# Layer 1, block 0: the causal mask added on TensorE, and one maximum for two heads

## The chip, the cores and the metric

The kernel runs on one core of one Trainium2 chip. Its time is the device time in microseconds (us) of one execution; the profile is of one execution more, whose own time is given beside its span, the time from its first to its last instruction. The engines are TensorE (PE for products, PEld for the loads of their stationary side), VectorE (DVE), ScalarE (ACT), GpSimd (POOL) and SyncE (SP), which issues most DMAs.

## What is computed

Two transformer layers over 2048 tokens of 128 channels. Layer 0 has attention of 16 heads without a mask and a mixture of 16 experts beside a shared one; layer 1 has causal attention of 8 heads with one set of keys and values for all, and a feed-forward part. The change is in layer 1's attention:

```python
k = x @ Wk
v = x @ Wv
q = jnp.einsum('btc,qcd->bqtd', x, Wq)
wei = jnp.einsum('bqtd,bsd->bqts', q, k) * scale
causal = jnp.tril(jnp.ones((t, t), dtype=bool))
wei = jnp.where(causal, wei, -jnp.inf)
wei = jax.nn.softmax(wei, axis=-1)
out = jnp.einsum('bqts,bsd->btqd', wei, v)
```

## The kernel before

Both attentions are made by one function, `attention` (from L319), which works in 4 blocks of 512 queries and, in each, in groups of 4 heads. A block and a group are a unit: layer 1 has 8 units, two to a block. Every unit goes through the keys twice.

The first pass finds the largest score of each query (`first_pass`, L396). One step (`step`, L402) takes a tile of 128 queries, a block of up to 512 keys and a pair of heads. Two products at L411 write the pair's scores into the two halves of a PSUM tile, one in the array's upper 64 rows and the other in its lower 64; the operands are in the reduced 32-bit format, with a high and a low part stacked along the rows. VectorE then takes the maxima. Where the keys lie wholly ahead of the queries, one plain reduction (L415) does both heads. Where the keys are of the queries' own block (`own`), the scores of later keys must not count. Then only the first n keys are multiplied, n being 128, 256, 384 or 512 for the four query tiles of a block, and each head gets an operation of its own at L420: it adds a strip of the constant `later` (L130 to L133), which is zero up to the diagonal and -2^100 after it, and takes the maximum. Its result comes through an accumulator, so that each L420 is followed by a short read of that accumulator. In block 0 every step is of this second kind, 8 steps to a unit.

The unit's maxima are then combined and negated (L426), split into a high and a low part (L436, L437), transposed on TensorE (L444) and copied by ScalarE (L445). The second pass (`second_pass`, L455) makes the scores again with keys as rows (L476), subtracts the maximum with one more product (L482), takes the exponential on ScalarE (L486), zeroes what lies after the diagonal on GpSimd (L489) and weighs the values on TensorE (L502).

PSUM tiles for scores come from one pool of three (`ps_s`), used by both passes in turn, so TensorE can be at most three pairs ahead of VectorE and ScalarE. The first pass of the next unit is woven into the second pass of the present one (`look_ahead`). In block 0 of layer 1 the first unit has nothing before it to be woven into: its 8 steps run with only the preparation of block 1 among them. This preparation is the keys (L295, finished by L296 and L297), the queries (L382, split at L272 and L273, and stacked by DMAs on SP's queue at L290) and the values (L1127, L1128).

Some stages carry an order written out by hand, but that ends with `ordered.close()` just ahead of layer 1's attention. From there on the build's scheduler decides how each engine's instructions stand. Constants are made at the start: `ident`, `later`, zeros and counters by GpSimd.

Of the kernel before, what the change touches and what calls it, by code (L numbers as in the profile page):

```python
# [11 lines left out]
F32R = mybir.dt.float32r  # L12
# [7 lines left out]
P = 128  # L20
T = 2048
NT = T // P
QB = 512
# [20 lines left out]
def two_layers(ctx: ExitStack, tc: tile.TileContext, a: dict, out: bass.AP):  # L44
    nc = tc.nc
    const = ctx.enter_context(tc.tile_pool(name="const", bufs=1))


    ident = const.tile([P, P], F32, name="ident")
# [67 lines left out]
    def gates(layer):  # L117
        for j in (2, 5):
# [11 lines left out]
    later = const.tile([P, QB], F32, name="later")  # L130
    nc.gpsimd.memset(later, 0.0)
    nc.gpsimd.affine_select(out=later, in_=later, compare_op=ALU.is_ge, fill=MASKED,
                            base=QB - P, pattern=[[-1, QB]], channel_multiplier=1)  # L133

    low = const.tile([P, 2, 2], F32, name="low")
    for i, at in enumerate((ident.rearrange("p (r c) -> p r c", c=4)[:, :, 2:4],
# [180 lines left out]
    def attention(layer, hT, ngrp, dk, scale, causal, kvp, begin, prepare, wq, bq, folded, ended,  # L317
# [23 lines left out]
        with ExitStack() as s:  # L341
# [10 lines left out]
            def other_bank():  # L352
                nonlocal others
                others += 1
                return banks[(weighing + 1 if fused or weighing >= 0 else others) % 2]
# [42 lines left out]
            def first_pass(u):  # L398

                b, grp = units[u]  # L400
                pm = qp.tile([P, TB, HG, NB], F32, name=f"{L}mx{u}", tag="mx")
                nkb = b + 1 if causal else NB  # L402

                def step(i, kb, pair):
                    own = causal and kb == b
                    n = (i + 1) * P if own else QB
                    ps = ps_s.tile([P, 2, QB], F32, name=f"{L}p1_{u}_{i}_{kb}_{pair}", tag="s")
                    for j in range(2):
                        g = 2 * pair + j
                        st, r = grp * nst + g // S, RT * (g % S)  # L410
                        nc.tensor.matmul(ps[:, j, :n], qS[b][r:r + RT, st, i * P:(i + 1) * P],  # L411
                                         kS(st)[r:r + RT, kb * QB:kb * QB + n],
                                         start=True, stop=True)
                    if not own:
                        nc.vector.tensor_reduce(pm[:, i, 2 * pair:2 * pair + 2, kb], ps,  # L415
                                                AX.X, ALU.max)
                    for j in range(2 if own else 0):

                        g = 2 * pair + j
                        nc.vector.tensor_tensor_reduce(  # L420
                            masked[:, :n], ps[:, j, :n], later[:, QB - n:], 1.0, LOWEST,
                            ALU.add, ALU.max, pm[:, i, g, kb:kb + 1])

                def largest():
                    nx = qp.tile([P, TB, HG], F32, name=f"{L}nx{u}", tag="nx")
                    nc.vector.tensor_reduce(nx, pm[:, :, :, :nkb], AX.X, ALU.max, negate=True)  # L426
                    nm = negmax[u % 2]
                    if fused:

                        parts = [(nm[:, :, :nm_rows].rearrange("p t (g w) -> p t g w", w=2), nx)]  # L430
                    else:

                        parts = [(nm.rearrange("p t (g w) -> p t g w", w=RT)[:, :, :, 2 * k:],
                                  nx[:, :, k * S:(k + 1) * S]) for k in range(nst)]
                    for v, nk in parts:
                        nc.vector.tensor_copy(v[:, :, :, 0].bitcast(F32R), nk)  # L436
                        nc.vector.tensor_tensor(v[:, :, :, 1], nk, v[:, :, :, 0], ALU.subtract)  # L437

                def turn():
                    nm = negmax[u % 2]  # L440
                    mT = qp.tile([nm_rows, QB], F32R, name=f"{L}mT{u}", tag="mT")
                    ps = other_bank()
                    for i in range(TB):
                        nc.tensor.transpose(ps[:, i * P:(i + 1) * P], nm[:, i, :], ident)  # L444
                    nc.scalar.copy(mT, ps[:nm_rows])  # L445
                    if fused:
                        for k in range(nst):
                            nc.sync.dma_start(
                                out=qS[b][31::32, grp * nst + k, :].bitcast(F32),
                                in_=mT[2 * S * k:2 * S * (k + 1), :].bitcast(F32))  # L450
                    shift[u] = mT

                steps = [(lambda i=i, kb=kb, pair=pair: step(i, kb, pair))
                         for i in range(TB) for kb in range(nkb) for pair in range(HG // 2)]
                last = steps.pop()  # L455
                return steps + [lambda: (last(), largest(), turns.append([0, turn]))]
# [837 lines left out]
```

## Time and profile before

| what | value |
|---|---|
| median of 3 runs | 1252.55 us (1251.54 to 1255.32) |
| the profiled execution | 1254.59 us |
| its span | 1252.9 us |
| TensorE products busy | 1156.8 us (92%) |
| VectorE busy | 943.9 us (75%) |
| ScalarE busy | 780.3 us (62%) |
| GpSimd busy | 94.4 us (8%) |
| mean granted TensorE clock | 0.944 |
| layer 1's first product at L411 | starts at 923.86 us |
| L420 in block 0 | from 924.56 to 947.3 us |

A line of a group names line, engine, operation, output and inputs with their shapes, how many there are, then the busy time and the mean of one in ns, and last how long the engine was idle just before them and what ended most of that. A line of a timeline has start, length, engine, line, operation and how many, and in brackets the idle time before it with its releaser. Products are pipelined and their ends are modelled: for them the distance from one start to the next says more than the listed length. The granted clock is the share of full speed at which TensorE may run.

### The profile page before, as it was taken

What the parts mean: (1) busy time and instruction counts of PE and PEld (TensorE: products, weight loads), DVE (VectorE), ACT (ScalarE), POOL (GpSimd) and SP (SyncE); (2) the same over time, 40 slices, a digit from 0 to 9 for tenths busy, and PEclk for the clock granted to TensorE, in tenths of its full rate; (3) what the DMA queues carried; (4) which work ended last, traced back from release to release, by engine and by line L of the source; (5) the groups of instructions that cost most, each with busy time, mean ns of one, the idle gap of its engine ahead of it and who ended that gap; (6) DMA issues with size and microseconds to landing.
All of it is one profiled execution on the core that took longest, in us unless ns stands there. A gap on an engine that the chain in (4) does not pass through costs nothing.

```text
span 1252.9 us, 22356 instructions
## 1 busy us (share of the span) xinstructions
PE 1156.8 (92%) x9230; PEld 523.6 (42%) x9230; DVE 943.9 (75%) x1462; ACT 780.3 (62%) x853; POOL 94.4 (8%) x157
## 2 busy tenths in 40 slices
PE   4579999999999999999999999979978989999985
PEld 2233434444343443443344333447734444444432
DVE  3888898889889889889889983343378788897134
ACT  6107777777777777777777778743333455656763
POOL 2002000000000000000000000320232011110113
PEclk9658999999999999999999999999977899999987
DMA  4841010203220213110000000032210101000001
GB/s 122 112 52 35 2 52 1 70 27 77 69 69 12 59 36 98 38 52 2 1 3 2 1 2 2 20 122 76 66 45 7 35 1 35 1 1 2 2 1 34
DMA packets 63094, 45.22 MB, mean 36 GB/s; under 512 B 6608, under 2 KB 56912, under 8 KB 62480
## 3 DMA queue, kind: packets, MB, share of 16 engines
q1 hardware_dynamic: 60224, 40.37, 13.2%
q0 software_dynamic: 1024, 2.10, 0.6%
q10 hardware_dynamic: 1744, 1.32, 0.6%
q8 instruction: 73, 1.20, 0.4%
q14 instruction: 29, 0.24, 0.1%
HBM read 9.88 MB, written 21.95 MB: 25 GB/s over the span
## 4 chain that ended last, share of the span: by engine, by line
PE 82%; DVE 10%; ACT 4%; issue 1%; DMA 1%; POOL 1%; ACTq 0%; POOLq 0%; DVEq 0%
PE a0bank L502 24%; PE a0p L476 17%; PE a0p L411 13%; PE a1bank L502 5%; PE a1p L476 4%; DVE a0mx L415 3%; DVE a1mx L415 2%; PE a1p L411 2%; PE a1p L482 2%; PE sg L991 2%; DVE a1masked L420 2%; ACT a0e L486 1%; PE gu L1043 1%; PE a0bank L533 1%; PE sum L979 1%
## 5 line engine op out<-in xcount | busy, mean ns | idle before, releaser
L415 DVE TENSOR_REDUCE a0mx<-a0p 128x2 f32<-128x1024 f32 x512 | 624.0, 1225 | 75.9 <-PE a0p L411 66.5
L486 ACT ACTIVATE a0e<-a0p 128x1024 f32<-128x1024 f32 x512 | 522.6, 1025 | 171.9 <-PE a0p L476 146.2
L502 PE MATMUL a0bank<-a0e,vA 128*32 128x256 f32 x4096 | 333.4, 392 | 0.8 <-ACT a0e L486 0.8
L411 PE MATMUL a0p<-kS,a0qS 64*128 64x512 f32 x1024 | 248.1, 480 | 24.7 <-DVE a0mx L415 13.0
L476 PE MATMUL a0p<-a0qS,kS 64*128 64x512 f32 x1024 | 260.6, 498 | 0.0
L486 ACT ACTIVATE a1e<-a1p 128x1024 f32<-128x1024 f32 (+3 forms) x160 | 143.1, 897 | 97.6 <-PE a1p L482 92.3
L476 PEld LDWEIGHTS a0p<-a0qS,kS 64*128 64x128 f32 x1024 | 97.3, 184 | 204.5 <-issue 128.7
L411 PEld LDWEIGHTS a0p<-kS,a0qS 64*128 64x128 f32 x1024 | 100.3, 192 | 109.4 <-ACT a0e L486 56.8
L502 PEld LDWEIGHTS a0bank<-a0e,vA 128*32 128x32 f32 x4096 | 86.4, 108 | 137.9 <-issue 124.4
L415 DVE TENSOR_REDUCE a1mx<-a1p 128x2 f32<-128x1024 f32 x96 | 115.8, 1222 | 17.8 <-PE a1p L411 17.2
L502 PE MATMUL a1bank<-a1e,vA 128*32 128x256 f32 (+1 forms) x1152 | 96.9, 385 | 0.4 <-POOL a1e L489 0.4
L476 PE MATMUL a1p<-a1qS,kS 64*128 64x512 f32 (+3 forms) x320 | 76.3, 463 | 4.9 <-DVE a1mx L415 3.7
L411 PE MATMUL a1p<-kS,a1qS 64*128 64x512 f32 (+3 forms) x320 | 67.7, 422 | 11.2 <-DVE a1mx L420 4.4
L420 DVE CUSTOM_DVE_ANT_0 a1masked<-a1p,later 128x128 f32<-128x128 f32 (+3 forms) x128 | 62.6, 489 | 13.4 <-PE a1p L411 7.5
L799 POOL DMA_INDIRECT sent<-hs,row_i x16 | 15.9, 995 | 712.6 <-DVE ln11xn L252 689.5
L482 PE MATMUL a1p<-a1mT,a1ones 64*128 64x512 f32 (+3 forms) x320 | 62.2, 375 | 0.0
L476 PEld LDWEIGHTS a1p<-a1qS,kS 64*128 64x128 f32 x320 | 31.5, 189 | 61.6 <-issue 32.3
L411 PEld LDWEIGHTS a1p<-kS,a1qS 64*128 64x128 f32 x320 | 32.2, 195 | 39.5 <-DVE a1mx L420 11.5
L489 POOL TENSOR_SCALAR_AFFINE_SELECT a1e<-a1e 128x256 f32<-128x256 f32 x64 | 26.0, 406 | 255.4 <-ACT a1e L486 255.4
L502 PEld LDWEIGHTS a1bank<-a1e,vA 128*32 128x32 f32 x1152 | 25.8, 109 | 42.8 <-issue 32.6
L445 ACT CAST a0mT<-a0bank 8x512 fp32r<-8x512 f32 x16 | 9.2, 576 | 45.4 <-PE a0bank L444 45.4
L482 PEld LDWEIGHTS a1p<-a1mT,a1ones 64*128 64x128 f32 x320 | 32.2, 193 | 2.3 <-issue 1.7
(340 smaller groups left out, 718.2 us busy)
## 6 DMA issues: line engine op xcount, KB each, us to landing
sent<-blank SPq DMA_DIRECT2D x68, 256.0 KB
kS<-a0qS SPq DMA_DIRECT2D x28, 128.0 KB
wgu_sb<-in_gate_up SPq DMA_DIRECT2D x1, 2048.0 KB
a0qS<-a0qh SPq DMA_DIRECT2D x62, 32.0 KB
a0qS<-a0ql SPq DMA_DIRECT2D x62, 32.0 KB
xs<-sent SPq DMA_DIRECT2D x31, 64.0 KB
y_rows<-y SPq DMA_DIRECT2D x7, 256.0 KB
a1qS<-a1qh SPq DMA_DIRECT2D x24, 64.0 KB
```

The source lines that it names most:

```text
L411: nc.tensor.matmul(ps[:, j, :n], qS[b][r:r + RT, st, i * P:(i + 1) * P], kS(st)[r:r + RT, kb * QB:kb * QB + n], start=True, stop=True)
L415: nc.vector.tensor_reduce(pm[:, i, 2 * pair:2 * pair + 2, kb], ps, AX.X, ALU.max)
L420: nc.vector.tensor_tensor_reduce(masked[:, :n], ps[:, j, :n], later[:, QB - n:], 1.0, LOWEST, ALU.add, ALU.max, pm[:, i, g, kb:kb + 1])
L476: nc.tensor.matmul(ps[:, j, q0:], kS(st)[r:r + RT, kt * P:(kt + 1) * P], qS[b][r:r + RT, st, q0:], start=True, stop=fused)
L482: nc.tensor.matmul(ps[:, j, q0:], ones[r:r + RT, g // S, :], shift[u][r:r + RT, q0:], start=False, stop=True)
L486: nc.scalar.activation(e[:, :, q0:], ps[:, :, q0:], AF.Exp, scale=scale)
L489: nc.gpsimd.affine_select(out=e[:, :, q0:q0 + P], in_=e[:, :, q0:q0 + P], compare_op=ALU.is_ge, fill=0.0, base=0, pattern=[[0, 2], [1, P]] ...
L502: nc.tensor.matmul(av[g * W:(g + 1) * W, c0:c1], vA(kt, grp * HG + g), held[kt, g // 2][:, g % 2, c0:c1], start=(kt == 0 and c0 == 0), sto ...
L533: nc.tensor.transpose(ps[:, i * P:(i + 1) * P], o[:, i * P:(i + 1) * P], ident)
L799: nc.gpsimd.indirect_dma_start(out=sent[t], in_=hs[:, i, :], in_offset=None, out_offset=bass.IndirectOffsetOnAxis(ap=row_i.bitcast(U32)[:, ...
L979: nc.tensor.matmul(sums[b][:, i * P:(i + 1) * P], act[:, i * P:(i + 1) * P], wsd[:, k, :], start=(k == 0 and i == 0), stop=(k == NS - 1), ...
L991: nc.tensor.matmul(ps[:, j, :], w[:, k * P:(k + 1) * P], hT[:, b * QB:(b + 1) * QB], start=True, stop=True)
```

## The change

Block 0 of layer 1 gets its mask on TensorE. Two constants are made at the start by copies on GpSimd: `later_r`, the last 128 columns of `later`, which hold the triangle, and `ident_r`, the identity, both in the reduced 32-bit format (their values survive it). In block 0 each head's product at L411 leaves its sum open, and a second product of identity and triangle adds the mask to the last 128 of the n columns; the columns ahead of these need none. The pair's maxima are then taken by one plain reduction over 2 x n elements, in place of two masked ones. Blocks 1 to 3 of layer 1 keep the masked operation, and layer 0 is as it was.

```diff
+    later_r = const.tile([P, P], F32R, name="later_r")
+    nc.gpsimd.tensor_copy(later_r, later[:, QB - P:])
+    ident_r = const.tile([P, P], F32R, name="ident_r")
+    nc.gpsimd.tensor_copy(ident_r, ident)
...
                         nc.tensor.matmul(ps[:, j, :n], qS[b][r:r + RT, st, i * P:(i + 1) * P],
                                          kS(st)[r:r + RT, kb * QB:kb * QB + n],
-                                         start=True, stop=True)
-                    if not own:
-                        nc.vector.tensor_reduce(pm[:, i, 2 * pair:2 * pair + 2, kb], ps,
+                                         start=True, stop=not (own and b == 0))
+                        if own and b == 0:
+
+                            nc.tensor.matmul(ps[:, j, n - P:n], ident_r, later_r,
+                                             start=False, stop=True)
+                    if not own or b == 0:
+                        nc.vector.tensor_reduce(pm[:, i, 2 * pair:2 * pair + 2, kb], ps[:, :, :n],
                                                 AX.X, ALU.max)
-                    for j in range(2 if own else 0):
+                    for j in range(2 if own and b > 0 else 0):
```

In the built program TensorE has 32 products more, each with a load of `ident_r`, all inside layer 1's block 0, where each follows the product at L411 whose sum it closes. VectorE has 16 plain maxima where it had 32 masked ones with 32 reads of the accumulator. Up to the end of block 0's first passes the other instructions keep their order on TensorE, but for some transposes and score products that stand a place earlier or later; a little after it, products of the first pass of block 1 and of the second pass of block 0 stand up to some eight places earlier or later against each other. GpSimd has the two copies near its start; SP's order is the same.

## The prediction

> **What bounds the kernel now.** I read first the page: its chain that ended last, and the two groups of maxima in layer 1.
>
> ```profile
> PE 82%; DVE 10%; ACT 4%; issue 1%; DMA 1%; POOL 1%; ACTq 0%; POOLq 0%; DVEq 0%
> ...
> L415 DVE TENSOR_REDUCE a1mx<-a1p 128x2 f32<-128x1024 f32 x96 | 115.8, 1222 | 17.8 <-PE a1p L411 17.2
> ...
> L420 DVE CUSTOM_DVE_ANT_0 a1masked<-a1p,later 128x128 f32<-128x128 f32 (+3 forms) x128 | 62.6, 489 | 13.4 <-PE a1p L411 7.5
> ```
>
> TensorE ends the chain over the whole kernel, but the share is an average; the change touches only 923.9 to 948 us. So I next read the chain in order of time in that stretch (start, us, what).
>
> ```profile
> 932.49 0.56 DVE a1masked L420
> 933.09 0.56 DVE a1masked L420
> 933.79 0.69 DVE a1masked L420
> 934.53 0.69 DVE a1masked L420
> 935.37 0.69 DVE a1masked L420
> 936.11 0.69 DVE a1masked L420
> ```
>
> Here the chain is VectorE: the masked maxima of block 0 follow one another, and from the timeline of TensorE in the same place:
>
> ```profile
> 935.28 0.48 PE L411 MATMUL a1p<-kS,a1qS 64*128 64x128 f32 x2 [1.10 <-DVE a1mx L420]
> 936.86 0.58 PE L411 MATMUL a1p<-kS,a1qS 64*128 64x256 f32 x2 [1.10 <-DVE a1mx L420]
> ```
>
> TensorE waits 1.1 us per pair of heads for VectorE to free one of three PSUM tiles. So VectorE's saving is on the path, and TensorE has room. How much room depends on its clock, which the busy times by stretch show (columns: length, then PE, PEld, DVE, ACT, POOL busy, then granted clock, DMA):
>
> ```profile
> 934.00:936.00 2.00, 0.66 (x4) 0.29 (x2) 1.82 (x6) 0.00 (x0) 0.00 (x0) 0.50 0.41 110
> 942.00:944.00 2.00, 1.77 (x10) 0.83 (x8) 1.60 (x7) 1.08 (x2) 0.65 (x2) 0.50 0.00 0
> 966.00:968.00 2.00, 2.00 (x7) 0.93 (x4) 1.77 (x6) 0.00 (x0) 1.27 (x1) 0.50 0.00 0
> ```
>
> TensorE runs at half speed for most of this stretch: 0.50 from 932.6 to 949.7, and at 926 to 929.
>
> **What is removed and what VectorE gains.** Block 0 has 2 units (groups of four heads) x 4 query tiles x 2 pairs = 16 pairs, four of each width n = 128, 256, 384, 512. A pair now costs two L420 operations, each with an accumulator read (83 ns), start to start 0.78, 1.05, 1.31 and 1.58 us in the timeline: 4 x 4.72 = 18.9 us. The plain maximum of 2 x 512 takes 1.225 us; L420 takes 0.691 at 512 and 0.288 at 128, so 1.05 ns an element on some 0.155 us. The plain ones of 2n elements are then (estimates from these rows) 0.43, 0.69, 0.96, 1.23 us: 4 x 3.31 = 13.2. VectorE gains 5.7 us, all on the path if nothing else becomes late.
>
> **What is added on TensorE.** In the order of the built program each product of 64 rows (L411) is now followed by one of 128 rows by 128 columns with `ident_r`, so a pair is own, mask, own, mask: 32 products and 32 weight loads. Streaming is little: 128 columns at 0.50 take 0.107 us (a 384 pair starts 0.32 us before the next one, so a column takes 0.83 ns at half clock, 0.42 at full). But two things are lost: the two heads of a pair, in the upper and lower 64 rows, now start within 3 ns of each other and no longer can; and each neighbour has another tile shape. What that costs is in the trace where layer 1 happens to alternate 64-row and 128-row products:
>
> ```profile
> 966.39 0.47 PE L259 MATMUL a1bank<-ident,ln22xn 128*128 128x128 f32 x1
> 966.80 0.58 PE L476 MATMUL a1p<-a1qS,kS 64*128 64x256 f32 x1
> 967.31 0.47 PE L259 MATMUL a1bank<-ident,ln22xn 128*128 128x128 f32 x1
> 967.71 0.58 PE L482 MATMUL a1p<-a1mT,a1ones 64*128 64x256 f32 x1
> 968.22 0.47 PE L259 MATMUL a1bank<-ident,ln22xn 128*128 128x128 f32 x1
> ```
>
> Start to start 0.51 after the 64-row product (256 columns stream in 0.213, so 0.30 is loading and change-over) and 0.40 after the 128-row one (its transposes repeat every 0.213 when among themselves, so 0.19). The mask in the reduced format streams 0.107, hence 0.30. A pair at half clock: 2 x (n/1.2 GHz + 0.30 + 0.30) = 1.40, 1.61, 1.83, 2.04 us. At full clock the same change-overs are 0.20 from a transpose to a 64-row product (L533 to L476, sixteen times) and 0.315 from a 512 pair to a transpose; a pair is about n/1.2 + 0.71 = 0.82, 0.93, 1.03, 1.14.
>
> Here a page speaks against the change: the Trainium skill, "TensorEngine Tiling (Array Packing)", Key Properties, says that moving to another tiling mode, not merely another tile, drains TensorE. It gives no figure; the rows above give 0.19 to 0.30. Without it a pair would be 2 x (n + 128)/1.2: 0.43 to 1.07, 12 us in all, and would hide under VectorE. With it the 16 pairs take 27.5 us, against 18.9 of VectorE's before. The sign hangs on this, and I take the rows.
>
> The second rule is on the clock: "TensorE: Matmul & The Clock Gate", Part 1, lets the full clock follow one busy window of about 3.4 us. If issuing without a gap counted as busy, the full clock would come after the first pairs and the 16 cost 15.7 us. The trace differs: from 966 to 970, in this very alternation, TensorE is listed busy for 2.00 and 1.66 of each 2 us, and still has 0.50 until 973.6. What streams there is under half of the time; in the new pairs it is (320 + 128)/1.2 = 0.37 of 0.86 us, 43%, alike. I take half clock from 925.8 on, as before, and also over 929 to 932.6, which was 1.0 before: the projections L295 and L382 that earned it are now diluted by mask pairs (about 2 of 3.4 us streaming; before 3).
>
> **The sum along TensorE's order.** From 923.86, where the first product starts:
> - first two pairs, full clock, 2 x 0.82: 925.5; L295 (block 1's keys) 1.5 as before: 927.0; two pairs of 256, 3.2: 930.2; L382 (block 1's queries) 1.9: 932.1; a 384 pair 1.83, L1127 (values) 1.9 at half clock (0.9 at full before), a 384 pair 1.83, two 512 pairs 4.08: 941.8. VectorE finished the unit's last maximum at 936.8 before.
> - second unit: pairs 1.40 x 2 + 1.61 x 2 + 1.83 x 2 + 2.04 x 2 = 13.8; between them, at half clock, block 0's second pass: L476 and L482 on 512 columns 4 x 0.43 and on 384 2 x 0.32, L444's transposes 1.05: 3.6 with a load in front. End: 959.1.
>
> Before, the last such product was done at 945.1 and VectorE took the first maximum of block 1 at 947.6. Now VectorE keeps no backlog but gets that tile only at about 961.6. That is 14.0 late; 1.0 comes back since L426, L436 and L437 of the second unit (0.17 + 0.46 + 0.25) stand ahead of it. **Net +13 us.** VectorE's 5.7 us turn into waiting for L411's tile and its mask.
>
> What is moved or hidden: behind the mask products stand L295, L382 and L1127 on TensorE, and behind the plain maxima stand VectorE's L297, L273 and L1128. They make block 1's operands; the eight DMAs L290 of its queries (930.1 to 940.2 now) start some 3 us later and end near 943, with block 1 not before 960: nothing. SP's order is unchanged. GpSimd's two copies of 128x128 at the start (some 0.3 us each, by its 128x128 select of 0.28) stand before a memset that ended at 8.05 and is first needed by a DMA at 27.4: nothing, and 0.6 if that cover of 19 us were gone. The change adds no other wait on them. After block 0 VectorE binds again (14.9 busy of 15 us from 950 to 965) and the order is nearly the same; the delay has nothing to fall into, since from 985 TensorE is 94% busy at full clock. Where the clock's windows fall over 963 to 984 may give or take 3 us.
>
> The profiled execution took 1254.59 us (span 1252.9 and 1.7 around it), so it would be 1267.6; it stands 2.0 above the median of the runs, 1252.55, to which I add the 13: **1265.5 us**.
>
> **Rivals.**
> - *Change-over as measured, at full clock part or all of the time.* All of it: 15.7 for the pairs, L295, L382 and L1127 3.1, second pass 2.3: 21.1 us, as long as the 21.2 now (923.86 to 945.1), with VectorE's backlog of about 2 gone: 1250.5. Half of the time: +5.5, 1258. For it: TensorE now has no gaps. Against: 966 to 973.
> - *Faster: the mask product is cheap and VectorE stays the bound.* If the accumulate into the same bank doesn't drain, the 5.7 come through less some 0.7 at the start: 1247.5. It decides where a pair costs TensorE less than about 0.87 us: 22.9 us of VectorE's stretch (924.6 to 947.5), less some 9 of other TensorE work (as listed above, with 1.1 of L502), over 16. For it: 1.1 us of idle per pair. Against: the change-over rows, constant to 0.01 us, ask 1.4 to 2.0. The lower end of the unknown cost is this, the upper end 0.10 more a pair for each load not overlapped, +3: 1268.5.
> - *Nothing moves.* A mixture near zero, 1250 to 1256.
>
> **How the numbers follow.** Half clock throughout, 1261.5 to 1269: 62%. Partly full clock, 1256 to 1261.5: 18%. Full clock or near zero, 1249 to 1256: 10%. Faster, below 1249: 10%. About 0.3% (3.8 us) is what a measurement of this kernel can tell from no change: slower than 1256.3 is 80%, within 10%, faster 10%. The range for 8 in 10 leaves out the gain and the tail above: 1254.5 to 1269.5.
>
> **What would show it.** Right: the mask's and L411's products alternate at 0.3 and 0.4 to 0.7 us, the clock reads 0.50 from 926 to about 962, VectorE idles before L415 on L411 or the mask, and block 1's first maximum starts near 961. Wrong: pairs under 1 us, clock 1.0 in that stretch, or TensorE still waiting for VectorE's maxima there.

## The result, and the profile after

The changed kernel takes 1272.66 us (median of 6 runs, 1271.45 to 1274.91), the kernel before in the same session 1253.07 (median of 6, 1251.54 to 1255.32). The ratio is 1.0156, 95% interval 1.0141 to 1.0172: slower by 19.6 us, where 13 were forecast. The direction and the mechanism came as forecast; the time lies 3.2 us above the range.

The profiled execution took 1271.45 us (span 1269.7, mean granted clock 0.936). On its page the chain that ended last and the two groups of maxima now read as follows. Lines have moved: L411 is L416, the mask product is L421, L415 is L424, L420 is L429, and the second pass's score product L476 is L485.

```profile
PE 83%; DVE 9%; ACT 4%; DMA 1%; issue 1%; POOL 1%; POOLq 0%; SPq 0%; ACTq 0%; DVEq 0%
...
L424 DVE TENSOR_REDUCE a1mx<-a1p 128x2 f32<-128x1024 f32 (+3 forms) x112 | 128.9, 1164 | 37.9 <-PE a1p L421 20.0
...
L429 DVE CUSTOM_DVE_ANT_0 a1masked<-a1p,later 128x128 f32<-128x128 f32 (+3 forms) x96 | 46.8, 488 | 8.1 <-PE a1p L416 4.7
```

VectorE is relieved as forecast: 32 masked maxima fewer (62.6 to 46.8 us, and 32 reads of 83 ns), 16 plain ones more (115.8 to 128.9), 5.4 us less in all. But it now idles 20.0 us ahead of the plain maxima, waiting for the mask product. The timeline of VectorE in block 0 shows such a wait ahead of each one:

```profile
941.67 1.23 DVE L424 TENSOR_REDUCE a1mx<-a1p 128x2 f32<-128x1024 f32 x1 [1.29 <-PE a1p L421]
943.92 1.23 DVE L424 TENSOR_REDUCE a1mx<-a1p 128x2 f32<-128x1024 f32 x1 [1.03 <-PE a1p L421]
```

The timeline of TensorE, after, shows what VectorE waits for. The first three lines are of the first pair, at full clock, the rest at half clock:

```profile
924.09 0.32 PE L416 MATMUL a1p<-kS,a1qS 64*128 64x128 f32 x1 [1.09 <-DVE a1qS L302]
924.34 0.33 PE L421 MATMUL a1p<-later_r,ident_r 128*128 128x128 f32 x1
924.60 0.32 PE L416 MATMUL a1p<-kS,a1qS 64*128 64x128 f32 x1
...
941.15 0.47 PE L421 MATMUL a1p<-later_r,ident_r 128*128 128x128 f32 x1
941.56 0.79 PE L416 MATMUL a1p<-kS,a1qS 64*128 64x512 f32 x1
942.28 0.47 PE L421 MATMUL a1p<-later_r,ident_r 128*128 128x128 f32 x1
942.69 0.79 PE L416 MATMUL a1p<-kS,a1qS 64*128 64x512 f32 x1
943.41 0.47 PE L421 MATMUL a1p<-later_r,ident_r 128*128 128x128 f32 x1
943.81 0.47 PE L416 MATMUL a1p<-kS,a1qS 64*128 64x128 f32 x1
944.22 0.47 PE L421 MATMUL a1p<-later_r,ident_r 128*128 128x128 f32 x1
```

Read the starts, not the listed lengths. At half clock it is 0.40 to 0.41 us from a mask product to the next start, 0.72 from a product of 512 columns and 0.40 to 0.41 from one of 128. A pair of 512 costs 2.25 us, and no two products start together any more. At full clock the steps of the first pair are 0.25 to 0.26, so a pair of 128 takes 1.03 us there and 1.61 at half clock.

The busy times by stretch, after (columns as in the prediction):

```profile
924.00:942.00 18.00, 17.91 (x41) 10.14 (x41) 6.19 (x11) 2.69 (x5) 0.00 (x0) 0.55 0.15 38
942.00:961.00 19.00, 19.00 (x50) 11.42 (x49) 7.90 (x14) 2.87 (x4) 0.82 (x2) 0.50 0.08 20
961.00:980.00 19.00, 16.86 (x116) 8.53 (x115) 16.26 (x54) 7.17 (x11) 3.73 (x9) 0.85 0.00 1
```

For 37 us TensorE has no gap, VectorE is busy 14 of the 37, and the clock stands at half: 1.0 for the first pairs only, then 0.50 from 925.8 to 966.8. Block 1's first plain maximum starts at 964.99, where it was 947.59: 17.4 us late. The first line is of before, the second of after:

```profile
947.59 1.23 DVE L415 TENSOR_REDUCE a1mx<-a1p 128x2 f32<-128x1024 f32 x1 [0.28 <-PE a1p L411]
964.99 1.23 DVE L424 TENSOR_REDUCE a1mx<-a1p 128x2 f32<-128x1024 f32 x1 [0.37 <-PE a1p L416]
```

From 972 us on, the profile after stays 16.9 to 17.0 us behind, by its exponentials and by its end.

### The profile page after: what moved, and what is told of

Same layout as the page of the kernel before. It is cut to its first block, busy times and chain, and to the rows that moved or that the text cites. A ratio compares the mean times of both kernels' runs of the same rounds, so it can differ in the third digit from the quotient of the medians.

```text
span 1269.7 us, 22361 instructions
## 1 busy us (share of the span) xinstructions
PE 1179.9 (93%) x9262; PEld 539.4 (42%) x9262; DVE 941.5 (74%) x1414; ACT 780.1 (61%) x853; POOL 95.1 (7%) x159
## 4 chain that ended last, share of the span: by engine, by line
PE 83%; DVE 9%; ACT 4%; DMA 1%; issue 1%; POOL 1%; POOLq 0%; SPq 0%; ACTq 0%; DVEq 0%
PE a0bank L511 23%; PE a0p L485 17%; PE a0p L416 12%; PE a1bank L511 5%; PE a1p L485 4%; PE a1p L416 3%; DVE a0mx L424 3%; PE a1p L491 2%; DVE a1mx L424 2%; PE sg L1000 2%; ACT a0e L495 1%; PE gu L1052 1%; DVE a1masked L429 1%; PE a1p L421 1%; PE a0bank L542 1%
## 5 line engine op out<-in xcount | busy, mean ns | idle before, releaser
L424 DVE TENSOR_REDUCE a0mx<-a0p 128x2 f32<-128x1024 f32 x512 | 623.9, 1224 | 74.8 <-PE a0p L416 65.1
L416 PE MATMUL a0p<-kS,a0qS 64*128 64x512 f32 x1024 | 248.0, 480 | 23.9 <-DVE a0mx L424 13.0
L485 PE MATMUL a0p<-a0qS,kS 64*128 64x512 f32 x1024 | 260.4, 497 | 0.0
L485 PEld LDWEIGHTS a0p<-a0qS,kS 64*128 64x128 f32 x1024 | 97.3, 184 | 204.5 <-issue 128.6
L424 DVE TENSOR_REDUCE a1mx<-a1p 128x2 f32<-128x1024 f32 (+3 forms) x112 | 128.9, 1164 | 37.9 <-PE a1p L421 20.0
L416 PEld LDWEIGHTS a0p<-kS,a0qS 64*128 64x128 f32 x1024 | 100.2, 192 | 108.7 <-ACT a0e L495 56.7
L416 PE MATMUL a1p<-kS,a1qS 64*128 64x512 f32 (+3 forms) x320 | 78.5, 430 | 7.0 <-ACT a1e L495 2.9
L485 PE MATMUL a1p<-a1qS,kS 64*128 64x512 f32 (+3 forms) x320 | 75.5, 463 | 4.3 <-DVE a1mx L424 3.7
L485 PEld LDWEIGHTS a1p<-a1qS,kS 64*128 64x128 f32 x320 | 31.3, 189 | 59.9 <-issue 33.2
L429 DVE CUSTOM_DVE_ANT_0 a1masked<-a1p,later 128x128 f32<-128x128 f32 (+3 forms) x96 | 46.8, 488 | 8.1 <-PE a1p L416 4.7
L416 PEld LDWEIGHTS a1p<-kS,a1qS 64*128 64x128 f32 x320 | 36.9, 197 | 36.8 <-ACT a1e L495 10.6
```

What stands on the lines that cost most here:

```text
L429: nc.vector.tensor_tensor_reduce(masked[:, :n], ps[:, j, :n], later[:, QB - n:], 1.0, LOWEST, ALU.add, ALU.max, pm[:, i, g, kb:kb + 1])
L485: nc.tensor.matmul(ps[:, j, q0:], kS(st)[r:r + RT, kt * P:(kt + 1) * P], qS[b][r:r + RT, st, q0:], start=True, stop=fused)
```

## The experiments

The theory: on TensorE each change between the 64-row product and the 128-row mask costs load and change-over, and that sum is what the kernel waits for. Its rivals were that the mask's work itself (32 products more, or the second write into an open sum) is the cost, and that VectorE's changed operations are. Eight kernels ran, each shown as its edit of the changed kernel unless said otherwise. "Before" was run beside them again: 1253.39 us for the first four (30 runs), 1253.58 for the others (27 runs). In each part what was expected comes first.

**The mask products stay, VectorE keeps its masked maxima.** The mask is added twice, which changes no maximum.

```diff
-                    if not own or b == 0:
+                    if not own:
...
-                    for j in range(2 if own and b > 0 else 0):
+                    for j in range(2 if own else 0):
```

> The mask products stay, and VectorE keeps the masked maxima of the kernel before (the mask is then added twice). Theory: each mask product costs TensorE two changes of tile shape, TensorE is the bound in block 0, and VectorE has about twice the time it needs; so the masked maxima hide and the time is that of the changed kernel, 1272 to 1275 us. First rival, that the plain maxima are what got slower or later: back near 1253. Second rival, that VectorE's 5.7 us were gained and lie inside a larger loss: 1278.

Measured: 1275.34 us (4 runs, 1274.0 to 1276.39), ratio 1.0182 (1.0163 to 1.0202). That is 0.3 above the range expected for the theory. So TensorE's part alone makes the loss. VectorE's whole saving is worth at most some 2.7 us beside it, not 5.4, and the intervals of the two ratios overlap, so that even this is not clear of the noise. VectorE waits for L421 in either kernel: 16.3 us in this one, 20.0 in the changed one.

**The plain maximum alone.** No mask products and no constants for them; block 0's maxima also run over later keys, which changes only what is subtracted from the scores ahead of the exponential, so the function stays the same.

```diff
-                                         start=True, stop=not (own and b == 0))
-                        if own and b == 0:
-
-                            nc.tensor.matmul(ps[:, j, n - P:n], ident_r, later_r,
-                                             start=False, stop=True)
+                                         start=True, stop=True)
```

> VectorE's half alone: one plain maximum for two heads in block 0, and no mask product. The maxima then run over later keys too; any bound from above serves the softmax as its shift, so the output is the same function. Theory: VectorE bounds block 0's first pass, so most of its 5.7 us come off: 1247 to 1250 us. Rival, that the stretch is held by something else (the chain over block 1's projections, or the granted clock): within 2 us of 1253.

Measured: 1253.57 us (14 runs, 1249.62 to 1255.75), ratio 0.9997 (0.9984 to 1.0010). The expected gain did not come, though the cost on TensorE is gone. Its own timeline of TensorE shows that VectorE still bound the first unit's end, where TensorE now waits 0.66 us a pair instead of 1.10:

```profile
933.68 0.48 PE L411 MATMUL a1p<-kS,a1qS 64*128 64x128 f32 x2 [0.66 <-DVE a1mx L415]
934.82 0.58 PE L411 MATMUL a1p<-kS,a1qS 64*128 64x256 f32 x2 [0.66 <-DVE a1mx L415]
```

The exponentials of block 0's second pass come earlier than before, the first by 1.4 us, those from 952 to 974 by 3.0 to 3.2. Then most of that is lost again. Busy times by stretch, first of the kernel before:

```profile
950.00:965.00 15.00, 11.79 (x92) 5.87 (x84) 14.87 (x56) 6.02 (x10) 2.84 (x7) 0.95 0.01 2
965.00:985.00 20.00, 17.69 (x74) 9.43 (x74) 10.22 (x34) 4.51 (x8) 2.90 (x5) 0.61 0.00 0
```

and then of this kernel:

```profile
950.00:965.00 15.00, 11.91 (x75) 5.74 (x71) 14.36 (x44) 4.92 (x7) 3.78 (x8) 0.82 0.01 2
965.00:985.00 20.00, 18.32 (x82) 9.37 (x81) 8.81 (x26) 4.31 (x8) 1.23 (x3) 0.54 0.00 1
```

The granted clock falls earlier (0.50 from 959.7 to 983.6 without a break, where before had a full window from 973.6 to 977.0) and by 986 only 1.3 us of the lead are left, at the last exponential of the attention 1.0, at the end of the kernel nothing. That the clock took the rest is read from these rows, not shown by an experiment.

**The mask product in the shape of its neighbours.** The same number of mask products in the same places, but each on the 64 rows of its head, so that it masks only the half of the queries whose rows these are; for the others later keys count in the maximum, which again changes only the shift.

```diff
-                            nc.tensor.matmul(ps[:, j, n - P:n], ident_r, later_r,
-                                             start=False, stop=True)
+                            nc.tensor.matmul(ps[:, j, n - P:n], ident_r[r:r + RT, :],
+                                             later_r[r:r + RT, :], start=False, stop=True)
```

> The mask product keeps its place and its 128 columns, but takes only the 64 rows of its head's own product, so that no tile shape changes (it masks half of the queries; the others' maxima run over later keys too). Theory, the change of shape is the cost: a pair costs TensorE at half clock at most 0.43 to 0.75 us with both heads again side by side, or about twice that if they are not, VectorE bounds again, and the time is 1247 to 1252 us. Rival, the added product itself is the cost (its load, or a second write to the same bank that must wait for the first): 1265 to 1273 us.

Measured: 1253.49 us (14 runs, 1244.56 to 1254.83), ratio 0.9994 (0.9976 to 1.0011). Of the 19.6 us nothing is left; the time is 1.5 above the range expected, since no gain came here either. Its timeline of TensorE at half clock:

```profile
940.05 0.80 PE L416 MATMUL a1p<-kS,a1qS 64*128 64x512 f32 x2
940.64 0.31 PE L421 MATMUL a1p<-later_r,ident_r 64*128 64x128 f32 x2
940.97 0.69 PE L485 MATMUL a1p<-a1qS,kS 64*128 64x384 f32 x2
```

"x2" means that the two heads' products stand side by side again; the pair of masks takes 0.33 us, and with the pair of 512 it is 0.92, not 2.25. As many added products, into the same open sums, are thus nearly free in the neighbours' shape, and the change of tile shape is the cost. Part of it is paid through the clock: this kernel has a mean of 0.80 to 0.81 from 924 to 950, where the changed one is at 0.50 after its first pairs. The two parts of the 19.6 us are not separated by a run; the price of a pair, 0.92 against 2.25 us, is compared at half clock.

**Both products, then both masks.** All of the masking, with half as many changes of shape.

```diff
-                        if own and b == 0:
-
-                            nc.tensor.matmul(ps[:, j, n - P:n], ident_r, later_r,
-                                             start=False, stop=True)
+                    for j in range(2 if own and b == 0 else 0):
+                        nc.tensor.matmul(ps[:, j, n - P:n], ident_r, later_r,
+                                         start=False, stop=True)
```

> The same 32 mask products of 128 rows, but a pair's two products at 64 rows come first and its two masks after: two changes of shape a pair and not four. Theory: a pair costs at half clock about n/1.2 GHz + 0.40 for the two heads side by side, 0.40 for the first mask and 0.2 for the second, 1.1 to 1.45 us where the changed kernel has 1.61 to 2.25, so some 10 us come back: 1261 to 1264 us. Rival, cost by the number of products and not of changes: the time of the changed kernel, 1272.

Measured: 1259.58 us (7 runs, 1255.11 to 1261.44), ratio 1.0046 (1.0030 to 1.0062). Its timeline of TensorE, in which the mask product is L420 (the second line shows the latter of the two masks of the first line by itself):

```profile
933.47 0.69 PE L420 MATMUL a1p<-later_r,ident_r 128*128 128x128 f32 x2
933.74 0.41 PE L420 MATMUL a1p<-later_r,ident_r 128*128 128x128 f32 x1
934.09 0.79 PE L416 MATMUL a1p<-kS,a1qS 64*128 64x512 f32 x2
934.81 0.69 PE L420 MATMUL a1p<-later_r,ident_r 128*128 128x128 f32 x2
935.43 0.79 PE L416 MATMUL a1p<-kS,a1qS 64*128 64x512 f32 x2
```

The two heads cost 0.72 us together, and two masks 0.62. From the first mask to the second it is 0.27, from the second to the next 64-row product 0.35; a mask with another shape on both sides takes 0.40, so the second one adds 0.21. A pair is 1.02, 1.13, 1.23 and 1.34 us by width, 18.9 us for all 16 at half clock. With the changed kernel's 1.61, 1.83, 2.04 and 2.25 (30.9 us) that is 12.0 less, and 13.1 came back, more than the 10 expected. The clock is at half in both, from about 925 on. Two thirds of the loss were the order of four products. About 6 us remain against before.

**The mask product made twice in succession.** The mask is added twice.

```diff
-                            nc.tensor.matmul(ps[:, j, n - P:n], ident_r, later_r,
-                                             start=False, stop=True)
+                            for again in range(2):
+                                nc.tensor.matmul(ps[:, j, n - P:n], ident_r, later_r,
+                                                 start=False, stop=(again == 1))
```

> The changed kernel with each mask product made twice in succession (the mask is added twice). Theory, the cost is the change of tile shape: the second stands behind a product of its own shape and costs 0.21 us at half clock, as the second mask of a pair did in the run with own, own, mask, mask: 32 x 0.21 = 6.8, so 1278 to 1281 us. Rival, every mask product costs its 0.40 us: 12.9, so 1285 us or more.

Measured: 1279.20 us (4 runs, 1273.64 to 1279.98), ratio 1.0203 (1.0173 to 1.0233). Twice the mask's work costs 6.5 us more, 0.20 a product, where the first of them costs 0.40 and splits the pair besides. In its timeline of TensorE, in which the mask product is L422, two masks in a row again take 0.61, from 940.86 to 941.47:

```profile
940.86 0.69 PE L422 MATMUL a1p<-later_r,ident_r 128*128 128x128 f32 x2
941.47 0.79 PE L416 MATMUL a1p<-kS,a1qS 64*128 64x512 f32 x1
```

**A filler against the half clock.** Twice, to see whether the clock took the gain of the plain maximum alone: four products of 512 columns ahead of each pair in the first unit, overwritten by the pair, once with that kernel and once with the kernel before.

```diff
+                    for j in (0, 1, 0, 1) if own and u == 0 else ():
+                        g = 2 * pair + j
+                        st, r = grp * nst + g // S, RT * (g % S)
+                        nc.tensor.matmul(ps[:, j, :], qS[b][r:r + RT, st, i * P:(i + 1) * P],
+                                         kS(st)[r:r + RT, :QB], start=True, stop=True)
```

> VectorE's half alone as before (plain maxima, no mask product), and in the first unit's first pass four idle-time products of 512 columns ahead of each pair, in the same 64-row shape, whose result the pair's own products overwrite. They do nothing but keep TensorE streaming. Theory: the 3 to 4 us that the plain maxima gain at the site are lost again where TensorE falls to half clock; with the filler the clock is full from about 933 to 960 us, block 0's second pass runs faster, and the time is 1246 to 1250 us. Rival, the clock is not what takes the gain back: 1253 us or more, since the filler is only more work.

> The kernel before with the same filler and its masked maxima as they were. Theory: VectorE binds the first unit, so the filler hides in TensorE's waits of 1.1 us a pair; what follows it runs at full clock sooner: 1249 to 1252 us. Rival, the granted clock does not matter in this stretch, since VectorE binds it: 1253 to 1256 us.

Measured: 1252.56 us (14 runs, 1248.42 to 1255.79), ratio 0.9999 (0.9985 to 1.0014), with the plain maximum; 1253.95 us (14 runs, 1249.45 to 1255.43), ratio 1.0010 (0.9995 to 1.0024), without. Both miss, and they don't decide it. Busy times by stretch with the plain maximum and the filler:

```profile
929.00:933.00 4.00, 2.43 (x18) 1.32 (x16) 4.00 (x9) 0.00 (x0) 0.00 (x0) 1.00 0.42 104
933.00:936.00 3.00, 2.67 (x10) 1.75 (x12) 1.32 (x5) 0.58 (x1) 0.00 (x0) 0.50 0.40 101
...
961.00:969.00 8.00, 6.96 (x18) 3.10 (x18) 4.10 (x11) 2.55 (x4) 1.57 (x3) 0.50 0.00 0
```

The filler held the full clock up to 933.0, for the first 12 us of block 0, whose first product stands at 920.91 in this profile; without the filler the clock is at half for 3.4 us of the first 9 and again from there on. But behind this stretch nothing moved. Counted from block 0's first product, the clock is at half from 36 to 60 us in both kernels, and all 160 exponentials of layer 1 lie within 0.2 us of their places. In the first row VectorE is busy for the whole 4.00 us, so a faster TensorE had nothing to give there. The filler thus did not change the clock where the gain goes, and these two runs leave open what takes it back. (This execution is 2.8 us shorter than that of the plain maximum alone, but it was ahead by as much at block 0's first product: its clock from 840 to 851 us is 1.00, that of the other 0.53.)

**The plain maximum in all four blocks.** No masked maximum and no mask product in layer 1; the maxima run over later keys of the block too, which changes the shift alone. The edit is of the kernel before:

```diff
-                    if not own:
-                        nc.vector.tensor_reduce(pm[:, i, 2 * pair:2 * pair + 2, kb], ps,
-                                                AX.X, ALU.max)
-                    for j in range(2 if own else 0):
+                    nc.vector.tensor_reduce(pm[:, i, 2 * pair:2 * pair + 2, kb], ps[:, :, :n],
+                                            AX.X, ALU.max)
+                    for j in range(0):
```

> One plain maximum for two heads in all four blocks of layer 1 and no mask for the maxima anywhere; they then run over later keys of the own block too, which only raises the softmax's shift. VectorE saves about 0.37 us for each of 64 pairs, 23 us. Theory: outside block 0 TensorE binds (94% busy at full clock from 985 us on), so little of it counts, and what block 0 gives has been taken back by the granted clock before: 1247 to 1253 us. Rival, that VectorE binds more of layer 1 than the busy shares show: below 1243 us.

Measured: 1246.07 us (6 runs, 1242.18 to 1247.02), ratio 0.9946 (0.9925 to 0.9967): faster than both kernels, and just below the range that was expected. Its group in the list of VectorE's work:

```profile
L414 DVE TENSOR_REDUCE a1mx<-a1p 128x2 f32<-128x1024 f32 (+3 forms) x160 | 166.6, 1061 | 33.4 <-PE a1p L411 31.6 <-ACT a1table L1159 0.8
```

64 plain maxima (166.6 less 115.8, so 50.8 us) stand where 128 masked ones and their reads were (62.6 and 10.6): VectorE does 22.4 us less, and a third of it, 7.5, reaches the end. Its profile, counted from block 0's first product, is 7.4 us ahead of before's at the fifth exponential of block 1, 5.1 at the last of that block, 7.8 at the last of layer 1 and 7.2 at the end of the kernel. A lead of the final size is thus made by the start of block 1's second pass, most of it behind 950 us, where VectorE was busy 14.87 of 15 us (950 to 965, in the row of before above). The mask is made in the second pass by GpSimd anyway. What it asks of the data is that no later key's score in the block lies so far above the largest allowed one that the exponentials of the allowed keys vanish.

## Why the prediction was right or wrong

- **VectorE bounds block 0 before: right, its worth too large.** VectorE was relieved by 5.4 us (5.7 forecast). "All on the path" was not so. Without any cost on TensorE the plain maximum alone gave some 3 us at the site and nothing measurable at the end, and the nearly free 64-row mask gave the same. The faster rival's 1247.5 would not have come even with a free mask.
- **TensorE becomes the bound by the change of tile shape: right.** The 64-row mask, which keeps the number of products and changes the shape, takes the whole loss away.
- **The 64-row product between others of another shape, n/1.2 GHz + 0.30 us: right.** Measured 0.40, 0.51, 0.62 and 0.72 us for 128 to 512 columns.
- **The mask product at 0.30 us: the failed step.** It measures 0.40 where the neighbours on both sides have another shape. The step took the 0.213 at which the transposes of 128 columns repeat among themselves as streaming, subtracted it from 0.40, and put 0.107 of streaming in its place. But the mask products, in the reduced format, repeat at 0.21 as well, where both neighbours have their shape (in the two runs with masks in a row). So the whole of the repeat belongs to the mask too, and 0.107 must not be put in its place. Whether the other half of the repeat is the load, or 128 rows that stream at half the pace, no run shows. The mask costs what the own product of 128 columns costs, and the row of 0.40 in the profile before could have been used as it stood. The term at full clock was too small in the same way: the first two pairs took 2.07 us, with the change to half clock near their end, where 1.64 was forecast. By their starts all 16 pairs took 28.9 us; the prediction's sum has 26.4 for them. That is 2.5 of the 3.4 us by which block 1's first maximum came later than the forecast 961.6. The rest is a start 0.2 later, 0.45 in L300 and 0.2 in the second pass's products and transposes between the pairs. (32 times the 0.107 that the term lacks is 3.4 too, but that is chance: four masks stand ahead of products of their own shape and take 0.27, and three of the 64-row products stand behind theirs and are shorter as well.)
- **Half clock from 925.8 to about 962: right**, to 966.8. The rival with the full clock fell: 37 us without a gap on TensorE at 0.50. L300 (block 1's keys) took 1.95 us where 1.5 was forecast, since it now lies at half clock as well; L387 and L1136 took 1.94 and 1.79, where 1.9 was forecast for each.
- **About 1 us returns: half of it.** 17.4 late at block 1's first maximum, 16.9 at the end.
- **From the profile to the median: the rest.** Between the two profiled executions it is 16.9 us, between the medians 19.6. The one before stands 1.5 above its median, the one after 1.2 below its own. The prediction moved the whole sum down by 2.0 for the first and could not know the second. Runs of one kernel fall into groups by their mean granted clock: before near 1249.5 us at 0.948 and near 1254 at 0.944, after 1271.5 to 1272.5 at 0.936 and 1272.9 to 1274.9 at 0.932.

So of the 6.6 us missed over the forecast 13, 2.5 are the price of the pairs, above all the mask product's size, 0.9 the other terms on TensorE, 0.5 the smaller return, and 2.7 the place of the profiled executions among their runs.

Open: what takes back the 3 us of the plain maximum alone; how much of the 19.6 us is the change of shape at a given clock and how much the half clock that lasts with it. A full mask in two 64-row products was not tried.

## What to carry to other kernels

Count the changes of tile shape on TensorE before adding a product, not the columns: one small product between two of another shape costs more than its columns (here 0.40 us at half clock for 128 columns), makes its neighbour pay too, and parts products that ran side by side. If it must be, put products of one shape together, and take a row that shows the whole step (load, change-over, streaming) instead of assembling it from parts. And ask first whether the masking is needed there: a maximum that only shifts an exponent may run over more keys than count, and leaving the mask out in all four blocks was the one version that gained.

## What was not expected of the hardware

- With another tile shape on both sides, a 64-row product of n columns takes n/1.2 GHz + 0.30 us at half clock, and the 128-row one of 128 columns the same 0.40. With its own shape on both sides the latter takes 0.21, ahead of its own shape alone 0.27, behind it alone 0.35. A 64-row pair side by side pays the 0.30 once (0.72 for two of 512).
- Listed as busy without a gap for 37 us, TensorE kept a granted clock of 0.50: by the formula above some 38% of the pairs' time was streaming (26% at 128 columns, 47% at 512; an estimate that takes 0.83 ns a column for the mask too). The Trainium skill, "TensorE: Matmul & The Clock Gate", Part 1, lets the full clock follow one busy window of some 3.4 us; these windows were busy by the profile's listing and did not earn it.
- Work taken from VectorE and work added to TensorE (the filler) both left the median within 0.1% of before, with the half-clock stretches shifted or lengthened. A few us saved in a stretch of changing clock are no safe gain.
